# A two-layer decoder with mixtures of experts: routing two more sets of tokens inside the second layer's attentions, and another order of chunks and quads in the last layer

## The chip, the cores and the metric

The kernel runs on one core of a Trainium2 chip. The metric is the time of one execution on the device in microseconds (us). It has five engines that work side by side, each with an instruction queue of its own: the matrix engine (PE; its weight loads are listed as PEld), the vector engine (DVE), the scalar engine (ACT), GpSimd (POOL) and the sync engine (SP), which here issues DMA transfers. ACT and POOL issue DMA transfers as well.

## The reference

A decoder of two layers works on 32 sequences of 128 tokens with 128 features (4096 tokens), beside a context of the same shape. Each layer adds three things to x in turn: self-attention, cross-attention to the context, and a feed-forward part. The change touches the feed-forward part of the second layer, a mixture of 16 experts of which every token uses 4, and a shared expert that all tokens use:

```python
router_logits = x @ gate_w.T
biased = router_logits + expert_bias
_, sel = lax.top_k(biased, TOP_K)                       # TOP_K = 4, E = 16
raw = jnp.take_along_axis(router_logits, sel, axis=-1)
rw = jax.nn.softmax(raw.astype(jnp.float32), axis=-1).astype(x.dtype)
g = jnp.zeros((T, E), x.dtype).at[jnp.arange(T)[:, None], sel].add(rw)
for e in range(E):
    routed = routed + g[:, e:e + 1] * _swiglu(x, w1[e], w2[e], w3[e])
out = (_swiglu(x, sw1, sw2, sw3) + routed).reshape(B, S, Hd)
```

Here x is the layer-normalized input, and `_swiglu` is silu(x w1) times (x w3), times w2. Everything is in float32.

## The kernel before

The 4096 tokens stay in on-chip memory as x in 8 *groups* of 512 (4 *batches* of 128 each). Two groups make a *set*, so there are four sets: 0 (groups 0, 1), 1 (2, 3), 2 (4, 5) and 3 (6, 7).

**Two ways through the experts.** Sets 0, 2 and 3 (`SETS`) are *sorted by expert*. For each token and each of its 4 experts the place of a row in a table in device memory is worked out (`Tables.route`, `placed`, `owned`). POOL scatters the rows there with indirect DMAs (`way_out`, line 2096, 32 for a set). The table has 48 tiles of 128 rows, worked on four at a time as 12 *quads* for each set, 36 in all: `rows_of` loads rows and the weights of the tiles' experts (SP; the table holds at most three quads' weights on chip), `rows_turned` transposes (tile prows), `rows_up` makes pg and pu and `rows_down` makes pyrows, which go back to device memory. Then POOL gathers the rows (`way_back`, tile back, 32 gathers for a set), and `added` adds them to x on DVE. Set 1, the *dense pair* of groups, goes through all 16 experts and the shared one instead: 17 *chunks* a group, 34 in all. A chunk is `chunk_up` (pg, pu, Silu on ACT, two products on DVE, the second with the token's *shares* of the expert, loaded by `fetched`) and `chunk_down` (y). For the six groups of the sorted sets one chunk each remains, the shared expert (`alone`). The last chunk of a group transposes x into y as well and stores the output.

**Stages before that.** A group is normalized by `norm` (statistics on DVE, line 1115, and r on POOL, lines 1097 and 1098) and `scaled` (line 1126), transposed by `turn` into the tile hx, and a set's logits are made by `routing`. `route` and `choose`/`chosen` go on with the choice of experts a few instructions at a time; for the dense pair `send` stores the shares in device memory.

**Where the order comes from.** `steps` (line 1188) lists stages with the step they begin at, how many steps lie between two runs of a stage, and how many runs there are. Each step goes through the first list in order; instructions of the stages in `between` are put in one by one after each of theirs. The order is fixed for PE, DVE, ACT and POOL, in the last layer for SP too. `second_layers` (line 2528 and on) has both attentions of the second layer interleaved over all groups; group g leaves the cross-attention at step 17 + 4g, the last at step 45. In it set 0 is normalized, routed and scattered too (`way_out` from step 35 on, one batch of 4 scatters a step). `last_layer` (line 2108 and on) does everything else: the dense pair's and set 2's norms, turns and routing in steps 0 to 5, quads from step 1 on, chunks from step 6 on (one in each step until step 23, then in every second one), then steps with two chunks, then those that stand alone. The dictionary `at` holds which chunks stand at which step.

Of the kernel before, what the change touches and what calls it, by code (L numbers as in the profile page):

```python
# [9 lines left out]
F32 = mybir.dt.float32  # L10
# [945 lines left out]
def fast_decoder(ctx: ExitStack, tc: tile.TileContext, ins, spans, out: bass.AP):  # L956
# [847 lines left out]
    def mixture(tag, W, route, per, last, weights_of, kept=lambda g: None):  # L1804
# [13 lines left out]
        def turn(wk, g):  # L1818
            pool = edge if g in groups(0) else wk
            hs[g] = pool.tile([128, GT], F32, name="hx", bufs=2 if g in groups(0) else 5)  # L1820
            by_feature(xn.pop(g), hs[g])

        def routing(wk, n):
# [4 lines left out]
            choices[n] = route(lg, edge)  # L1828
# [74 lines left out]
        made = {"hs": hs, "combs": combs, "weights": weights, "NS": NS}  # L1903
# [56 lines left out]
    class Tables:  # L1960
# [32 lines left out]
        def kept(self, g):  # L1993
            self.xn[g] = self.spare[:, g]
            return self.xn[g]
# [97 lines left out]
        def way_out(self, n, u):  # L2093
            b, g = u % GB, n * NBR // GB + u // GB
            for k in range(4):
# [12 lines left out]
    def last_layer(tag, W, stages, of_expert, tables):  # L2108

        wk = phase(tag, mixture_psum)  # L2110
        tables.later(wk)
        send, made = stages[5], stages[-1]
        hs, shares, NS = made["hs"], {}, made["NS"]
        xn, places, parts, owners = tables.xn, tables.places, tables.parts, tables.owners
        factors, choices, held, ys, sgs, outs = ({} for _ in range(6))
# [5 lines left out]
        def scaled(g):  # L2121
            xn[g] = wk.tile([128, GB, D], F32, name="xr", bufs=6)
            yield from normed(wk, g, *factors.pop(g), xn[g], nc.vector)

        def turn(g):
            hs[g] = wk.tile([128, GT], F32, name="hx", bufs=NG - 2)
            by_feature(xn[g], hs[g])
# [10 lines left out]
        def routing(n):  # L2138
# [4 lines left out]
            choices[n] = tables.route(lg, n) if n in SETS else route_softmax(lg, edge)  # L2143
            next(choices[n])

        def chosen(n):
            comb = yield from choices.pop(n)
            if comb is not None:
                made["combs"][n] = comb
# [100 lines left out]

        at, todo = {}, list(dense)
        for s in range(6, NQ + 1):
            if s < 2 * QUADS or s % 2 == 0:
                at[s] = [todo.pop(0)]
        for s in range(NQ + 2, 100):
            if not todo:
                break
            at[s] = [todo.pop(0) for _ in range(min(2, len(todo)))]
        for k in range(0, 4, 2):
            at[s + k // 2] = alone[k : k + 2]  # L2260
        at[s + 3], at[s + 5] = alone[4:5], alone[5:6]
        LAST = s + 6
# [3 lines left out]
        for before, g in zip([None, *dense_groups], dense_groups):  # L2266
            for j in range(E // NS):
                fetches.append(((g, j), 5 if before is None else step_of[before, NS * j + NS - 1] + 1))
# [11 lines left out]
        def downs(s):  # L2280
            while waiting and (len(at.get(s, ())) < 2 or not at.get(s + 1)):
# [6 lines left out]
        def several(stage, keys):  # L2288
            def run(_):
# [5 lines left out]
        dense_n = ({1, 2, 3} - set(SETS)).pop()  # L2295
        n2, n3 = SETS[1:]
        batches = lambda n: [(n, u) for u in range(NBR)]
        once = lambda stage, k, s: (lambda _: stage(k), s, 1, 1)
# [3 lines left out]
            (each(rows_turned, quads), 1, 1, NQ),  # L2302
            (several(turn, of_set(dense_n)), 2, 1, 1),
            once(routing, dense_n, 2),
            (lambda _: send(wk, dense_n), 4, 1, 1),
            (several(turn, of_set(n2)), 4, 1, 1),
            once(routing, n2, 4),
            once(tables.owned, n2, 8),
            (several(turn, of_set(n3)), 10, 1, 1),
            once(routing, n3, 10),  # L2310
            once(tables.owned, n3, 14),
            (ups, 0, 1, LAST),
            (each(rows_down, quads), 2, 1, NQ),
            (each(rows_up, quads), 1, 1, NQ),
# [3 lines left out]
                (each(rows_of, quads[2:]), 1, 1, NQ - 2),  # L2318
# [360 lines left out]
```

## Time and profile before

| what | us |
|---|---|
| median of 3 runs (lowest, highest) | 1415.12 (1402.57, 1415.6) |
| the profiled execution's own time | 1410.02 |
| its span, first to last instruction | 1408.2 |
| mean granted clock of PE in it | 0.947 |
| busy in the span: PE, DVE, ACT, POOL | 1259.3, 858.3, 577.2, 534.6 |
| last instruction chain's largest shares | PE 64%, DVE 15%, POOL 7%, DMA 5% |
| bytes moved by DMA | 129.06 MB |

The profile is one execution. An engine is busy while one of its instructions runs; matmuls are pipelined and their ends are modelled. A matmul in float32 stands as two records in the profile. The granted clock is the share of its full clock that PE was given. DMA share is the mean busy share of the core's 16 DMA engines. A line such as "engine line waited for" gives the total of the waits, how many there were, and the longest. In the chain each line has its start, its length, and the engine, tile and line.

### The profile page before, as it was taken

What the parts mean: (1) busy time and instruction counts of PE and PEld (TensorE: products, weight loads), DVE (VectorE), ACT (ScalarE), POOL (GpSimd) and SP (SyncE); (2) the same over time, 40 slices, a digit from 0 to 9 for tenths busy, and PEclk for the clock granted to TensorE, in tenths of its full rate; (3) what the DMA queues carried; (4) which work ended last, traced back from release to release, by engine and by line L of the source; (5) the groups of instructions that cost most, each with busy time, mean ns of one, the idle gap of its engine ahead of it and who ended that gap; (6) DMA issues with size and microseconds to landing.
All of it is one profiled execution on the core that took longest, in us unless ns stands there. A gap on an engine that the chain in (4) does not pass through costs nothing.

```text
span 1408.2 us, 27520 instructions
## 1 busy us (share of the span) xinstructions
PE 1259.3 (89%) x10753; PEld 846.7 (60%) x10753; DVE 858.3 (61%) x2271; ACT 577.2 (41%) x848; POOL 534.6 (38%) x729
## 2 busy tenths in 40 slices
PE   3689999999999999699999988989986688799997
PEld 2357777777777787444444445656653376577753
DVE  5646767676777575385775536666674346534563
ACT  1354445454554433133232235555543434334432
POOL 5233243435341231032000214444427605575775
PEclk8789999999999999799999999989987869999999
DMA  9501111121111111455055020000001259599943
GB/s 351 177 1 32 32 31 33 32 50 34 41 31 32 32 32 37 92 112 122 14 107 122 0 97 1 3 1 2 2 1 31 84 156 334 193 337 306 326 147 96
DMA packets 89528, 129.06 MB, mean 92 GB/s; under 512 B 9872, under 2 KB 63760, under 8 KB 87984
## 3 DMA queue, kind: packets, MB, share of 16 engines
q1 hardware_dynamic: 76624, 102.59, 26.0%
q0 software_dynamic: 6144, 12.60, 3.0%
q10 hardware_dynamic: 6624, 12.05, 2.3%
q8 instruction: 87, 1.43, 0.4%
q14 instruction: 49, 0.40, 0.1%
HBM read 99.34 MB, written 27.85 MB: 90 GB/s over the span
## 4 chain that ended last, share of the span: by engine, by line
PE 64%; DVE 15%; POOL 7%; DMA 5%; ACT 4%; issue 3%; SPq 1%; DVEq 0%; ACTq 0%; POOLq 0%
PE po L977 8%; PE pg L977 7%; PE pu L977 7%; PE y L977 6%; PE pqk L977 6%; PE scores L977 4%; PE sums L977 4%; PE xscores L977 3%; POOL rows_in L2096 3%; PE pval L977 3%; DMA factor<-factors 2%; PE pyrows L977 2%; PE proj L977 2%; PE xsums L977 2%; PE qkvr L977 2%
## 5 line engine op out<-in xcount | busy, mean ns | idle before, releaser
L1280 ACT ACTIVATE e<-scores 128x1024 f32<-128x1024 f32 x128 | 124.0, 1021 | 61.5 <-PE scores L977 61.5
L977 PE MATMUL y<-sg,wide 128*128 128x512 f32 x224 | 117.6, 613 | 7.5 <-DVE sg L2229 2.6
L977 PE MATMUL pg<-hx,wide 128*128 128x512 f32 x224 | 116.0, 599 | 0.0
L977 PE MATMUL pu<-hx,wide 128*128 128x512 f32 x224 | 115.3, 596 | 0.0
L2204 POOL DMA_INDIRECT back<-rows_out,place x96 | 93.1, 970 | 37.5 <-issue 24.6
L1295 DVE STREAM_TRANSPOSE by_token<-sums 128x512 f32<-128x512 f32 x64 | 45.6, 713 | 96.7 <-PE sums L977 96.5
L1126 POOL TENSOR_SCALAR xn<-x,mv,r 128x128 f32<-128x128 f32 x80 | 67.7, 853 | 91.7 <-PE pxn L1135 82.8
L1097 POOL TENSOR_SCALAR r<-mv 128x4 f32<-128x4 f32 x48 | 11.5, 241 | 219.4 <-DVE mv L1116 219.0
L1531 ACT ACTIVATE e<-xscores 128x1024 f32<-128x1024 f32 x64 | 62.0, 1021 | 79.9 <-PE xscores L977 79.9
L1882 ACT ACTIVATE sg<-pg 128x512 f32<-128x512 f32 x72 | 43.0, 597 | 119.4 <-PE pg L977 110.4
L977 PE MATMUL sums<-e,v 128*32 128x128 f32 x2048 | 74.8, 290 | 17.2 <-POOL v L1075 17.1
L977 PE MATMUL scores<-qb,k 32*128 32x512 f32 x512 | 79.1, 689 | 11.9 <-ACT qb L1466 4.5
L1883 DVE TENSOR_TENSOR sg<-sg,pu 128x512 f32<-128x512 f32 x72 | 49.3, 685 | 61.1 <-PE pu L977 58.1
L1097 POOL TENSOR_SCALAR r2x<-mv 128x2 f32<-128x2 f32 x16 | 3.7, 234 | 212.0 <-DVE mv L1116 212.0
L977 PEld LDWEIGHTS sums<-e,v 128*32 128x32 f32 x2048 | 55.7, 115 | 46.8 <-POOL v L1075 21.6
L2096 POOL DMA_INDIRECT rows_in<-xr,place x64 | 62.9, 983 | 34.6 <-issue 18.0
L1545 DVE COPY v<-pval 128x512 f32<-128x512 f32 x64 | 43.5, 680 | 51.1 <-PE pval L977 51.1
L1579 ACT COPY av<-po 128x512 f32<-128x512 f32 x64 | 37.5, 586 | 89.6 <-PE po L977 89.5
L977 PEld LDWEIGHTS pu<-hx,wide 128*128 128x128 f32 x224 | 42.6, 191 | 52.5 <-issue 50.1
L977 PE MATMUL po<-e,v 128*64 128x128 f32 x1024 | 65.8, 281 | 8.2 <-DVE v L1545 8.2
L977 PE MATMUL po<-av,wide 128*128 128x256 f32 x256 | 64.1, 405 | 8.1 <-DVE av L1599 8.1
L977 PEld LDWEIGHTS y<-sg,wide 128*128 128x128 f32 x224 | 35.9, 189 | 58.0 <-DVE sg L1885 36.7
(300 smaller groups left out, 2913.2 us busy)
## 6 DMA issues: line engine op xcount, KB each, us to landing
row_weights<-in_w1f_dram SPq DMA_DIRECT2D x144, 192.0 KB, 4.2
factor<-factors SPq DMA_DIRECT2D x64, 256.0 KB, 5.0
share<-combined SPq DMA_DIRECT2D x32, 512.0 KB, 11.4
rows_in<-in_few SPq DMA_DIRECT2D x36, 256.0 KB, 4.1
rows<-rows_in SPq DMA_DIRECT2D x36, 256.0 KB, 5.3
rows_out<-yrows ACTq DMA_DIRECT2D x36, 256.0 KB, 4.3
share<-combined SPq DMA_DIRECT2D x8, 1024.0 KB, 7.8
wide<-in_w1f_dram SPq DMA_DIRECT2D x1, 3272.0 KB, 10.5
```

The source lines that it names most:

```text
L977: last[0] = nc.tensor.matmul(*args, **kw)
L1097: nc.gpsimd.tensor_scalar(t, src, add, None, ALU.add)
L1126: eng.tensor_scalar(n[:, b, :], x[g][:, b, :], mv[:, b, 0:1], r[:, b : b + 1], ALU.subtract, ALU.mult)
L1280: nc.scalar.activation(e[-1], ps[:, bass.ts(n, 2)].rearrange("p c i s -> p (c i) s"), AF.Exp, scale=scale)
L1295: nc.vector.transpose(tt.rearrange("p i t r -> p (i t r)"), po.rearrange("p i s -> p (i s)"))
L1531: nc.scalar.activation(e[-1], ps[:, n].rearrange("p r c s -> p (r c) s"), AF.Exp, scale=scale)
L1545: nc.vector.tensor_copy(v[:, bass.ts(n, XC), :], pv)
L1579: nc.scalar.copy(avs[w][n][:, :, bass.ts(b, S)], po)
L1882: nc.scalar.activation(sg, pg, AF.Silu)
L1883: nc.vector.tensor_tensor(sg, sg, pu, ALU.mult)
L2096: sent = nc.gpsimd.indirect_dma_start(out=rows_in[n], out_offset=bass.IndirectOffsetOnAxis(ap=self.places[n][:, k, u : u + 1], axis=0), in ...
L2204: nc.gpsimd.indirect_dma_start(out=outs[n, u][:, k], out_offset=None, in_=rows_out[n], in_offset=bass.IndirectOffsetOnAxis(ap=places[n][:, ...
```

## The change

Five things change.

1. In `second_layers` the stages `rnorm`, `rscaled` and `rturn` run for groups 0 to 5 and not only 0 and 1 (steps 18 + 4g to 20 + 4g); `routing` runs for sets 0, 1 and 2 (steps 25, 33, 41), the dense pair's choice is completed in steps 34 to 39 and sent at step 41. Turned inputs of groups 2 to 5 are kept in four context tiles that are no longer read (`cx`), and set 2's normalized rows in two more.
2. The scatters of set 0 go three to a step over steps 35 to 45, not four to a step over 35 to 42.
3. In `last_layer` the stages of 1 are gone for sets 1 and 2, except for set 2's choice and places (steps 0, 1) and its scatters, now two batches a step from step 2 on. Set 3's norm, turn, routing and scatters stand at steps 3 to 16.
4. The order of chunks: two in each of steps 0 to 2, one in each of steps 3 to 8, one in every second step from 9 to 29; the quads begin at step Q = 3. From step 40 on the other 11 chunks of the pair and four shared ones stand one to a step, and the two last shared ones at steps 55 and 59. The first shares are fetched at step 0, before the first quads' rows.
5. `downs` leaves two chunks waiting in steps 0 to 2 and 40 to 57. The last set's gathers stand at every second step.

```diff
-    def mixture(tag, W, route, per, last, weights_of, kept=lambda g: None):
+    def mixture(tag, W, route, per, last, weights_of, more={}, kept=lambda g: None):
...
-            pool = edge if g in groups(0) else wk
-            hs[g] = pool.tile([128, GT], F32, name="hx", bufs=2 if g in groups(0) else 5)
+            pool, bufs = (edge, 2) if g in groups(0) else (wk, 5)
+            hs[g] = more[g] if g in more else pool.tile([128, GT], F32, name="hx", bufs=bufs)
...
         def kept(self, g):
-            self.xn[g] = self.spare[:, g]
-            return self.xn[g]
+            if g < 2:
+                self.xn[g] = self.spare[:, g]
+            elif g * GB // NBR in SETS:
+                self.xn[g] = cx[g - 2].rearrange("p (b f) -> p b f", f=D)
+            return self.xn.get(g)
...
         def scaled(g):
-            xn[g] = wk.tile([128, GB, D], F32, name="xr", bufs=6)
+            xn[g] = wk.tile([128, GB, D], F32, name="xr", bufs=2)
...
-            hs[g] = wk.tile([128, GT], F32, name="hx", bufs=NG - 2)
+            hs[g] = wk.tile([128, GT], F32, name="hx", bufs=2)
...
+        Q = 3
+        many = {**{s: 2 for s in range(Q)}, **{s: 1 for s in range(Q, Q + 6)}, **{s: 1 for s in range(Q + 6, Q + 28, 2)}}
         at, todo = {}, list(dense)
-        for s in range(6, NQ + 1):
-            if s < 2 * QUADS or s % 2 == 0:
-                at[s] = [todo.pop(0)]
-        for s in range(NQ + 2, 100):
-            if not todo:
-                break
-            at[s] = [todo.pop(0) for _ in range(min(2, len(todo)))]
-        for k in range(0, 4, 2):
-            at[s + k // 2] = alone[k : k + 2]
-        at[s + 3], at[s + 5] = alone[4:5], alone[5:6]
-        LAST = s + 6
+        for s, n in many.items():
+            at[s] = [todo.pop(0) for _ in range(n)]
+        END = NQ + Q + 1
+        for s, item in enumerate(todo + alone[0:4], END):
+            at[s] = [item]
+        at[s + 1], at[END + 19] = alone[4:5], alone[5:6]
+        LAST = END + 21
...
         def downs(s):
-            while waiting and (len(at.get(s, ())) < 2 or not at.get(s + 1)):
+
+            while len(waiting) > (2 if s < Q or END <= s < LAST - 3 else 0):
                 chunk_down(*waiting.pop(0))
                 yield
...
-            (each(rows_turned, quads), 1, 1, NQ),
-            (several(turn, of_set(dense_n)), 2, 1, 1),
-            once(routing, dense_n, 2),
-            (lambda _: send(wk, dense_n), 4, 1, 1),
-            (several(turn, of_set(n2)), 4, 1, 1),
-            once(routing, n2, 4),
-            once(tables.owned, n2, 8),
-            (several(turn, of_set(n3)), 10, 1, 1),
-            once(routing, n3, 10),
-            once(tables.owned, n3, 14),
+            (each(rows_turned, quads), Q, 1, NQ),
+            (several(turn, of_set(n3)), 6, 1, 1),
+            once(routing, n3, 6),
+            once(tables.owned, n2, 3),
+            once(tables.owned, n3, 11),
...
-                once(chosen, n2, 5),
-                once(several(norm, of_set(n3)), None, 5),
-                once(tables.placed, n2, 6),
-                *((each(tables.way_out, batches(n2)[i::2]), 7, 1, 4) for i in range(2)),
-                once(several(scaled, of_set(n3)), None, 8),
-                once(chosen, n3, 11),
-                once(tables.placed, n3, 12),
-                (each(tables.way_out, batches(n3)), 13, 1, NBR),
-                (each(way_back, batches(0)), 21, 1, NBR),
-                (each(added, batches(0)), 24, 1, NBR),
+                once(chosen, n2, 0),
+                once(tables.placed, n2, 1),
+                (each(tables.way_out, to_send(n2, 2)), 2, 1, 4),
+                once(several(norm, of_set(n3)), None, 3),
+                once(several(scaled, of_set(n3)), None, 4),
+                once(chosen, n3, 7),
+                once(tables.placed, n3, 8),
+                (each(tables.way_out, to_send(n3, 1)), 9, 1, NBR),
+                (each(way_back, batches(0)), 19, 1, NBR),
+                (each(added, batches(0)), 22, 1, NBR),
...
-                (each(way_back, batches(n3)), NQ + 3, 1, NBR),
-                (each(added, batches(n3)), NQ + 5, 1, NBR),
+                (each(way_back, batches(n3)), END + 1, 2, NBR),
+                (each(added, batches(n3)), END + 4, 2, NBR),
...
-            (first(rturn), 20, 4, R),
+            (first(rturn), 20, 4, 3 * R),
...
-            (first(routing), 25, 1, 1),
+            (first(routing), (25, 33, 41), 1, 3),
             (lambda _: tables.owned(0), 36, 1, 1),
+            (lambda _: send(early, 1), 41, 1, 1),
...
-                (first(rscaled), 19, 4, R, xturn),
-                (first(rnorm), 18, 4, R),
+                (first(rscaled), 19, 4, 3 * R, xturn),
+                (first(rnorm), 18, 4, 3 * R),
...
-                (lambda u: tables.way_out(0, u), 35, 1, NBR),
+                (lambda i: tables.way_out(0, to_send[3 * i : 3 * i + 3]), 35, 1, 11),
+                (lambda _: choose(1, 3), 34, 1, 6),
...
-        mixture1 = mixture("l1f", W1F, lambda lg, _: tables.route(lg, 0), 1, True, of_expert, tables.kept)
+        route = lambda lg, n: tables.route(lg, n) if n in SETS else route_softmax(lg, edge)
+        mixture1 = mixture("l1f", W1F, route, 1, True, of_expert, {2: cx[0], 3: cx[1], 4: cx[4], 5: cx[5]}, tables.kept)
```

## What was predicted

> **What bounds the kernel now.** I read the page first, then busy time by stretches, then the chain of work that ended last, then the waits. On the page the matrix engine is busy for most of the span:
>
> ```profile
> PE 1259.3 (89%) x10753; PEld 846.7 (60%) x10753; DVE 858.3 (61%) x2271; ACT 577.2 (41%) x848; POOL 534.6 (38%) x729
> ```
>
> That is an average over stages with different limits. The same figures by stretches of layer 1 (columns: stretch, its length, busy time of each engine, granted clock, DMA share, GB/s):
>
> ```profile
> core 0: us, PE busy (x) PEld busy (x) DVE busy (x) ACT busy (x) POOL busy (x), PEclk, DMA share, GB/s
> 830.00:1038.00 208.00, 190.79 (x2394) 126.45 (x2394) 139.46 (x392) 112.13 (x157) 90.89 (x138) 0.96 0.01 2
> 1038.00:1069.00 31.00, 24.37 (x284) 16.11 (x284) 20.58 (x58) 9.76 (x12) 10.73 (x14) 0.78 0.04 13
> 1069.00:1117.00 48.00, 26.99 (x345) 15.23 (x345) 18.98 (x61) 19.45 (x22) 36.92 (x48) 0.86 0.12 38
> 1117.00:1165.00 48.00, 39.27 (x231) 35.45 (x224) 20.31 (x83) 17.07 (x25) 3.73 (x7) 0.68 0.59 175
> 1165.00:1207.00 42.00, 38.82 (x238) 28.97 (x237) 25.71 (x83) 17.95 (x29) 25.60 (x28) 1.00 0.91 327
> 1207.00:1222.00 15.00, 7.70 (x49) 5.98 (x50) 5.20 (x16) 3.17 (x5) 8.46 (x9) 0.91 0.22 66
> 1222.00:1290.00 68.00, 66.91 (x388) 48.70 (x388) 27.02 (x50) 26.90 (x46) 42.76 (x44) 0.97 0.97 321
> 1290.00:1352.00 62.00, 60.60 (x412) 48.99 (x411) 37.68 (x86) 27.16 (x46) 45.51 (x48) 1.00 0.95 307
> 1352.00:1408.00 56.00, 45.85 (x148) 23.25 (x146) 29.00 (x64) 13.64 (x23) 36.17 (x37) 0.96 0.29 83
> ```
>
> The attentions end about 1117 (steps 33 to 45 are 1038 to 1117); the last layer follows. Until 1038 PE is the limit. From 1038 to 1117 nothing is full: PE is busy 51 of 79 us. The last layer opens badly (1117 to 1165: clock 0.68, DMA 0.59) and has a hole at 1207 to 1222 (DMA 0.22), where the second set's rows are still being scattered. From 1222 to 1352 the DMA engines are full (0.97, 0.95). The chain shows a step of that stretch, one quad and one chunk:
>
> ```profile
> 1250.97 0.89 PE pyrows L977 x8
> 1251.86 0.89 PE pg L977 x8
> 1252.76 0.89 PE pu L977 x8
> 1253.65 0.86 PE y L977 x2
> 1254.95 0.86 PE pg L977 x2
> 1256.66 0.89 PE pyrows L977 x8
> ```
>
> A chunk is pg, pu and y: 3 x 0.86 = 2.58 us. A quad is its transposes (0.44, what is left between y and pg) and 3 x 0.89: 3.11. Together 5.69, the distance of the two pyrows. In the waits of 1038 to 1118, PE stands behind POOL's queue, which the scatters fill:
>
> ```profile
> PEld sums L977 <- POOL v L1075: 10.8, 6, 3.9
> PE pxn L1135 <- POOL xn L1126: 5.2, 1, 5.2
> ```
>
> **Part 1: what moves into the attentions.** For each of groups 2 to 5, from the timeline: statistics 4 x (0.26 + 0.18) = 1.8 us of DVE; r 0.23 + 1.04 = 1.3 of POOL; normalizing 0.6 of DVE and 1.6 of POOL (in the last layer it was 1.1 of DVE); four transposes 0.66 of PE and a copy 0.58 of ACT. Twice the logits: 1.85 of PE at full clock, 3.60 at half. The dense pair's routing: 3.9 of DVE in some 18 instructions and one Exp; send: 0.9 of PE at full clock, two copies of 0.57, two small DMAs. Sum: PE 4 x 0.66 + 2 x 1.85 + 0.9 = 7.2 (13 at half clock), DVE 4 x 2.4 + 3.9 = 13.5, POOL 4 x 2.9 = 11.6, ACT 3.8. Not all is new there: twelve statistics run at 1075 to 1081, where the attention's own norm has four, so eight of the last layer (3.5 of DVE, 2.6 of POOL) were already ahead of its start, in front of the r that the 5.2 us wait of pxn hangs on.
>
> Groups 2 and 3 fall into steps 26 to 32, where PE is the limit (191 of 208): two turns there cost 1.3; DVE and POOL have a third and a half of the time free and hide the rest. In steps 33 to 45 come groups 4 and 5, both logits, the routing and send: PE 5.9, of which I put 3 on the path, as PE idles a third of the time; DVE 2 x 2.4 + 3.9 - 3.5 = 5.2, put on the path whole, because the norms stand in DVE's queue ahead of the transposes that PE waits for. POOL: 5.8 - 2.6 added, but at 3 scatters a step instead of 4, steps 35 to 42 carry 24 instead of 32, 8 x 1.26 less (spacing of scatters, 0.96 and 0.3 issue). A quarter of the 16 us of waits behind POOL goes: -4. Sum 1.3 + 3 + 5.2 - 4 = +5. Bounds: -8 (POOL's relief alone, half of its waits) to +27 (PE at half clock and DVE, all on the path). The attentions then end at 1122. The last scatters of set 0 now end after the attentions (steps 43 to 45), but the first rows are wanted only in step 3.
>
> **Part 2: the opening.** Steps 0 to 2 are six chunks, 15.5 us of PE that wait for no rows. They need the shares: four fetches of 1 MB, now ahead of the quads on SP, with two quads of 1.05 MB: 6.3 MB. At the rate of a full DMA, (64.0 MB moved from 1117 to 1352 over 195 us of share, 0.329 MB/us), 19 us. The last layer's first 48 us now have a clock of 0.68. How long a low clock lasts (the same columns):
>
> ```profile
> 1146.00:1157.40 11.40, 11.31 (x52) 10.19 (x53) 0.29 (x1) 4.23 (x7) 0.00 (x0) 0.50 0.20 48
> ```
>
> PE was busy all the 11.4 us and stayed at half. Again so: +5.7, 21 us in all. Beneath it DVE does the second set's routing and places (5.0 of work at 1153 to 1166, 6 for set 0's places at 1038 to 1049), 11 us, and six chunks' products, 6 x 1.38: 19 us, just hidden; what DVE holds up there is the second set's scatter, which then starts about 24 us in, ends 8 x 5.04 = 40 later at 64, and is wanted at step 13 (21 + 40 + 4 x 5.1 = 81). The hole at 1207 goes; this slack of 17 us is the cover. A rule of the Trainium skill (TensorE: Matmul & The Clock Gate, Part 1) says that about 3.4 us of sustained work restores the clock; by it the 5.7 would be 1.7, 4 us less. The row above disagrees, and the sum goes by the row.
>
> **Part 3: the middle.** Steps 3 to 8, a quad and a chunk each: 6 x 5.69 = 34, and the third set's turn and logits 3.2 and two placings of 1.9: 41; I write 40. DMA there: 10 MB, 30 us, so PE binds. Steps 9 to 38 hold 30 quads and 11 chunks: PE 30 x 3.11 + 11 x 2.58 = 122. DMA: a quad moves 0.79 of weights, 0.26 in and 0.26 out, 1.31 MB; 30 of them 39.3, shares 4.2, one scatter and two gathers of 2.1 each: 49.8 MB, 151 us. DMA binds, so the quads without chunks near the end (steps 31 to 38) run at about 4.8 (1.31 and a gather's 0.26 MB at 0.329) and not at 3.11. Last quad: 21 + 40 + 151 = 212. Counting otherwise, 195 us of DMA share plus 13 in which PE holds it up: 208. I take 210 after 1122; before it was 235 after 1117. Bounds: 186 (PE alone, with no DMA wait: 17 + 41 + 122 + 6 for what is added to x) and 224 (the hole's 15 us comes back). The Trainium skill (DMA: Bandwidth & Descriptors, Anatomy of one DMA) gives transfers a slope of 436 GB/s; by it 49.8 MB would take 114 us and PE would bind at 122, 29 us earlier. This trace at full share shows 329, and 393 at most in any ten us.
>
> The second group's share fetches wait on SP for their buffer, with quad loads behind them; before, SP's waits on shares were 5.9 us in all, covered by two quads loaded ahead. Nothing is charged.
>
> **Part 4: the end.** After the last quad stand 17 chunks instead of 15: 43.9, and x's transposes 8 x 0.89 = 7.1: 51.0 of PE (before 45.8, from 1352 to 1398). From there to the end were 10.5: last gather, sum, copy, store. So 61.5. POOL alone: rows stored 4.3, 32 gathers 40.3, 9 from the last one's end: 53.6, under it. Keeping chunks two behind costs nothing: Silu 0.60 and two products of 0.69 lie under the next two chunks' 3.4 of pg and pu.
>
> **Sum.** 1122 + 210 + 61.5 = 1393.5 of span, 1395 with the 1.8 around it, against 1410.0 of the profiled execution. The three runs lie on both sides of that (1402.6 to 1415.6, median 1415.1), so I carry no shift: 1395.
>
> **Rivals.**
> - DMA does not bind and the clock opens fast (the 186): 1122 + 186 + 61.5 + 1.8 = 1371. For it: ten-us stretches with 393 GB/s. Against: 130 us at 0.96 share.
> - The gain is hidden: DVE's queue puts all moved work on the path (+27 instead of +5), or the second set's scatter starts over 17 us late and the hole returns (+14): 1409 to 1417. For it: DVE is in order and holds products that wait for shares.
> - The other side: PE stands 5 us more often in steps 33 to 45, because turns and logits in PE's queue wait for POOL's normalizing behind scatters. Each such stand drops the clock: 5 + 5.7 = 10.7. Two eat the gain, four make it slower by 1% (1395 + 43 = 1438). For it: the waits of pxn and sums above, and 0.78 and 0.86 of clock. Against: POOL has less to do in these steps.
>
> **How the numbers follow.** Under 1401 or over 1429 is what a measurement of this kernel can tell from no change. Forecast 0.50 (own range 1380 to 1408); first rival 0.14; second 0.20; third 0.16. Under 1401: three quarters of the forecast, the first rival and a little of the second, 0.55. Over 1429: most of the third, 0.15. Between: 0.30. The range leaves out a third of the first rival below (0.05) and what is over 1430 (0.15): 1368 to 1430.
>
> **What would show it.** Right: pg<-hx of group 2 ahead of any prows; DMA share near 0.95 from the opening to the last quad with no hole; last quad about 210 after the attentions' end; that end within 1114 to 1149. Wrong: first scatter of set 2 later than 40 us in; PE under half busy in steps 33 to 45; quads of steps 31 to 38 at 3.1 apart (then DMA was no bound).

## The result and the profile after

| | before | after |
|---|---|---|
| median of 20 runs each (us) | 1415.32 (1402.57 to 1421.91) | 1422.58 (1410.38 to 1430.83) |
| ratio, 95% interval | | 1.0059 (1.0032 to 1.0086) |
| the profiled execution: its own time, span, granted clock | 1410.02, 1408.2, 0.947 | 1417.03, 1414.8, 0.954 |
| attentions of layer 1, from the first pkphi to the last proj with w1x | 294.4 | 298.1 |
| from there to the last pyrows, the last quad's end | 231.8 | 232.2 |
| from there to the end of the span | 56.3 | 57.3 |

The kernel became 0.6% slower; 1.1% faster was forecast against the profiled execution (1395 for 1410.02). The time lies in the stated range (1368 to 1430), but the forecast gain of the last layer is not there: it takes 289.5 us after the attentions, 288.1 before.

The first line of the page is as good as unchanged; busy time doesn't tell where the gain went:

```profile
PE 1259.1 (89%) x10753; PEld 843.4 (60%) x10753; DVE 852.7 (60%) x2263; ACT 575.3 (41%) x846; POOL 539.8 (38%) x737
```

The stretches of the last layer tell it. The attentions now end at 1125.3 (same columns as before: stretch, length, busy time of five engines, granted clock, DMA share, GB/s):

```profile
core 0: us, PE busy (x) PEld busy (x) DVE busy (x) ACT busy (x) POOL busy (x), PEclk, DMA share, GB/s
1125.00:1148.00 23.00, 19.53 (x52) 10.16 (x53) 14.04 (x39) 6.38 (x9) 5.64 (x7) 0.85 0.86 304
1148.00:1161.00 13.00, 12.51 (x66) 8.35 (x65) 10.37 (x33) 4.15 (x7) 9.39 (x10) 1.00 0.65 215
1161.00:1181.00 20.00, 11.54 (x63) 8.74 (x61) 4.42 (x12) 4.12 (x7) 15.86 (x18) 0.74 0.64 218
1181.00:1200.00 19.00, 17.72 (x113) 13.59 (x113) 10.77 (x36) 8.69 (x14) 8.73 (x9) 1.00 0.59 182
1200.00:1247.00 47.00, 44.19 (x300) 35.70 (x298) 17.92 (x37) 20.01 (x34) 31.56 (x33) 1.00 0.98 323
1247.00:1310.00 63.00, 57.56 (x371) 47.26 (x372) 26.41 (x56) 24.82 (x42) 34.28 (x37) 0.95 0.93 293
1310.00:1350.00 40.00, 30.02 (x222) 25.68 (x221) 14.48 (x36) 13.62 (x24) 25.58 (x27) 1.00 0.97 313
1350.00:1358.00 8.00, 7.15 (x45) 6.34 (x44) 4.01 (x10) 2.52 (x5) 0.00 (x0) 0.79 0.27 100
1358.00:1415.00 57.00, 50.04 (x158) 25.33 (x156) 28.97 (x59) 14.63 (x25) 31.54 (x32) 0.97 0.25 75
```

The opening (1125 to 1148) is near what was foreseen, clock 0.85 and DMA 0.86 where before had 0.68 and 0.59. From 1200 to 1350, when the quads' loads are nearly over, the DMA engines are full (0.93 to 0.98), also as foreseen. In between is a new hole: for 52 us, from 1148 to 1200, DMA moves at 0.59 to 0.65, and in its middle PE is busy 11.5 of 20 us at a clock of 0.74, while POOL is busy 15.9. The old hole at 1207 to 1222 is gone, and this one stands in its place.

What POOL does there, and who waits, is in the timeline of that stretch (start, length, engine, line, operation; in brackets the idle time before it and what ended it):

```profile
1156.89 0.18 DVE L1116 BATCH_NORM_AGGREGATE mv<-parts 128x2 f32<-128x6 f32 x1
...
1168.33 0.96 POOL L2100 DMA_INDIRECT rows_in<-ctx,place  x1 [0.30 <-issue]
1169.31 0.26 POOL L1097 TENSOR_SCALAR r<-mv 128x4 f32<-128x4 f32 x1
1169.65 1.05 POOL L1098 TENSOR_TENSOR r<-r,half 128x4 f32<-128x4 f32 x1
...
1170.73 1.12 DVE L1126 TENSOR_SCALAR xr<-x,mv,r 128x128 f32<-128x128 f32 x4 [9.48 <-POOL r L1098]
...
1173.86 0.69 DVE L2232 TENSOR_TENSOR sg<-sg,share 128x512 f32<-128x512 f32 x1
...
1174.61 1.22 PE L977 MATMUL y<-sg,wide 128*128 128x512 f32 x1 [8.46 <-DVE sg L2232]
```

Read it from the top. Set 3's norm (step 3) has its statistics on DVE by 1157.1. The next thing it needs, r, is two instructions on POOL, 1.3 us together for a group. They are queued behind set 2's scatters, two batches a step since step 2, and scatters follow each other every 1.26 us: r begins at 1169.3, 12 us after its input was ready. Its reader, `scaled` of step 4, is one step behind `norm`, so DVE reaches it early and stands 9.5 us for it. DVE's order is fixed, and behind `scaled` stand the chunks' products, the first of which follows it at 1173.2: y has no sg, PE stands 8.5 us. Then quads come late, their buffers come free late, and SP's weight loads wait for pyrows, 14.8 us at the longest. The same as totals of waits from 1125 to 1360 (engine, line, what it waited for: us in all, how many, the longest):

```profile
DVE xr L1126 <- POOL r L1098: 9.7, 2, 9.5
PE y L977 <- DVE sg L2232: 9.4, 2, 8.5
```

In before, set 3's `norm` stood at step 5, ahead of set 2's scatters (from step 7 on), and `scaled` at step 8, three steps after it.

### The profile page after: what moved, and what is told of

It is laid out like the page before. It is cut to its first block, busy times and chain, and to the rows that moved or that the text cites. A ratio compares the mean times of both kernels' runs of the same rounds, so it can differ in the third digit from the quotient of the medians.

```text
span 1414.8 us, 27530 instructions
## 1 busy us (share of the span) xinstructions
PE 1259.1 (89%) x10753; PEld 843.4 (60%) x10753; DVE 852.7 (60%) x2263; ACT 575.3 (41%) x846; POOL 539.8 (38%) x737
## 4 chain that ended last, share of the span: by engine, by line
PE 62%; DVE 16%; DMA 8%; POOL 5%; ACT 4%; issue 3%; SPq 1%; DVEq 0%; ACTq 0%; POOLq 0%
PE po L977 8%; PE pg L977 7%; PE pu L977 6%; PE y L977 6%; PE pqk L977 6%; PE scores L977 5%; PE sums L977 4%; DMA row_weights<-in_w1f_dram 4%; PE xscores L977 3%; PE pval L977 3%; DMA factor<-factors 2%; PE proj L977 2%; PE xsums L977 2%; ACT e L1280 2%; PE qkvr L977 2%
## 5 line engine op out<-in xcount | busy, mean ns | idle before, releaser
L1126 POOL TENSOR_SCALAR xn<-x,mv,r 128x128 f32<-128x128 f32 x84 | 71.1, 854 | 91.3 <-PE pxn L1135 82.7
L977 PE MATMUL pg<-hx,wide 128*128 128x512 f32 x152 | 78.0, 595 | 0.0
L977 PE MATMUL pu<-hx,wide 128*128 128x512 f32 x152 | 77.7, 593 | 0.0
L2192 DVE TENSOR_TENSOR sgrows<-sgrows,pu 128x512 f32<-128x512 f32 x36 | 24.7, 687 | 86.2 <-PE pu L977 85.4
L1579 ACT COPY av<-po 128x512 f32<-128x512 f32 x64 | 37.6, 587 | 89.0 <-PE po L977 88.9
L1510 DVE COPY qk<-pqk 128x512 f32<-128x512 f32 x64 | 43.4, 685 | 41.1 <-PE pqk L977 40.9
## 6 DMA issues: line engine op xcount, KB each, us to landing
wide<-in_w1f_dram SPq DMA_DIRECT2D x1, 3272.0 KB, 10.7
```

The source lines that it names most:

```text
L977: last[0] = nc.tensor.matmul(*args, **kw)
L1126: eng.tensor_scalar(n[:, b, :], x[g][:, b, :], mv[:, b, 0:1], r[:, b : b + 1], ALU.subtract, ALU.mult)
L1510: nc.vector.tensor_copy(t, ps)
L1579: nc.scalar.copy(avs[w][n][:, :, bass.ts(b, S)], po)
L2192: nc.vector.tensor_tensor(sg, sg, pu, ALU.mult)
```

## The experiments

**The theory** after this comparison: the middle is bound by DMA as predicted, and the loss is the queue in front of r. **Its rivals**: the DMA engines would have delivered the last quad no earlier without that stand; the attentions, not the last layer, eat the gain; the order of chunks is worth nothing.

Each edit is to the changed kernel unless it says otherwise. A count that orders all of them is the start of the copy `hrows` on ACT, one for each quad, in us after the attentions' end. It splits the time to the last pyrows into the prediction's terms: the first quad; quads 0 to 5 (steps 3 to 8); from quad 6 to the last quad's end.

| kernel | attentions | first quad | quads 0 to 5 | quad 6 to the last pyrows | last pyrows | end after it | ratio to before, 95% interval |
|---|---|---|---|---|---|---|---|
| predicted | +5 | 21 | 40 | 151 | 210 | 61.5 | |
| after | 298.1 | 23.5 | 53.2 | 155.5 | 232.2 | 57.3 | 1.0059 (1.0032 to 1.0086) |
| e1 norm first | 306.4 | 23.4 | 42.5 | 155.6 | 221.5 | 56.9 | 0.9968 (0.9932 to 1.0003) |
| e2 scaled late | 306.3 | 23.7 | 35.7 | 165.4 | 224.8 | 57.0 | 1.0013 (0.9974 to 1.0053) |
| e3 one batch a step | 302.1 | 23.7 | 43.2 | 154.1 | 221.0 | 56.9 | 0.9993 (0.9956 to 1.0031) |
| e4 four scatters | 301.3 | 21.8 | 54.6 | 154.3 | 230.7 | 57.0 | 1.0086 (1.0053 to 1.0119) |
| e5 few chunks first | 302.1 | 15.7 | - | - | 225.7 | 57.0 | 1.0006 (0.9969 to 1.0042) |
| e6 half the weight loads | 302.1 | 23.8 | 42.5 | 133.5 | 199.8 | 57.4 | 0.9805 (0.9744 to 0.9867) |
| e7 set 2 back | 303.1 | 32.4 | 49.8 | 154.8 | 237.0 | 57.0 | 1.0087 (1.0051 to 1.0123) |
| e8 spread | 306.3 | 23.7 | 43.2 | 153.2 | 220.1 | 57.8 | 0.9977 (0.9946 to 1.0009) |
| e9 before again | 291.0 | - | - | - | 232.8 | 56.1 | 0.9995 (0.9959 to 1.0032) |
| e10 even | 306.3 | 23.7 | 35.8 | 159.6 | 219.1 | 57.2 | 0.9957 (0.9928 to 0.9986) |
| e11 even, one batch | 306.4 | 23.5 | 37.2 | 158.7 | 219.4 | 57.4 | 0.9981 (0.9947 to 1.0015) |
| e12 norms later | 293.9 | 23.5 | 38.3 | 159.8 | 221.6 | 56.9 | 0.9981 (0.9943 to 1.0019) |

Times of stretches are of one profiled execution each; ratios are of 10 to 20 timed runs (4 for e6). A dash stands where the quads begin at other steps. The attentions' column differs by up to 8 us between kernels whose attentions are the same (after, e1 to e3, e5, e6, e8, e10, e11); the columns of the last layer are the ones to compare.

### e1: r ahead of the scatters

```diff
                 once(chosen, n2, 0),
+                once(several(norm, of_set(n3)), None, 0),
...
-                once(several(norm, of_set(n3)), None, 3),
```

> The changed kernel with one line moved: set 3's norm stands at step 0 of the last layer instead of step 3, so its r is in POOL's queue ahead of set 2's 32 scatters. Queue theory: in the changed kernel r ran at 1169, 12 us after its statistics, behind 16 scatters; DVE stood 9.5 us for it, PE 8.5 us behind DVE, then some 6 us at half clock, and SP's loads stood 14.8 us. All of that goes: the last quad comes 12 to 18 us earlier after the attentions' end (232 us becomes 214 to 220), the time falls by 10 to 18 us against the changed kernel, to 0.993 to 0.999 of the kernel before. Rival, DMA is the bound whatever waits: the hole closes, the same bytes are still in the way, the last quad stays within 4 us of 232 and the ratio within 0.003 of 1.006.

The same stretches, counted from the attentions' end of this kernel (1139.4):

```profile
1175.40:1195.40 20.00, 19.76 (x126) 15.08 (x125) 8.95 (x25) 8.89 (x15) 15.12 (x17) 1.00 0.93 297
1195.40:1214.40 19.00, 16.74 (x112) 13.29 (x111) 13.21 (x43) 8.05 (x14) 10.85 (x12) 1.00 0.81 275
```

In the first of these PE is busy 19.8 of 20 us at full clock instead of 11.5 at 0.74, and DMA is at 0.93 instead of 0.64, with POOL as busy as before (15.1): the scatters did not shrink, r only no longer stands behind them. Six quads take 42.5 us instead of 53.2, the last quad ends 10.7 us earlier, and nothing is given back after quad 6 (155.6 and 155.5). It is a little less than the 12 to 18 us expected. Where one stage of two groups stands in a queue is worth 0.9% of the whole kernel.

### e2 and e3: the same stand taken away in two other ways

In e2 r stays behind the scatters, but set 3's readers come four steps later. In e3 the scatters are thinned to one batch a step.

```diff
-                once(several(scaled, of_set(n3)), None, 4),
+                once(several(scaled, of_set(n3)), None, 8),
```

> The changed kernel with set 3's norm left at step 3 (its r still behind 16 scatters on POOL), but what reads r moved from step 4 to step 8, with turn and logits at step 10 and choice, places and scatters 4 steps later too. Queue theory: r is as late as before, but by step 8 it is there, so neither DVE nor PE waits; the gain is that of the run with the norm first, within 4 us, if the third set's later scatters (steps 13 to 20) don't collide with set 0's gathers from step 19 on. Rival, it is the scatters themselves that slow everything beside them (DMA or descriptors): r is no matter, and the stretch of the 32 scatters stays as slow as in the changed kernel, ratio about 1.006.

```diff
-                (each(tables.way_out, to_send(n2, 2)), 2, 1, 4),
+                (each(tables.way_out, to_send(n2, 1)), 2, 1, NBR),
```

> The changed kernel with set 2's scatters at one batch (4) a step over steps 2 to 9 instead of two batches a step over 2 to 5; the norm stays at step 3. Queue theory: 8 scatters and not 16 stand before r, 10 us less of POOL's queue (8 x 1.26), so r comes about when its statistics are done plus 2 us, and DVE's wait falls from 9.5 us to under 2; most of the gain of the run with the norm first, 8 to 16 us against the changed kernel. But the scatters of set 3 stand at step 9 and may queue. Rival, DMA is the bound: no change from 1.006.

(e2 moves set 3's turn, choice, places and scatters by four steps too.) In e2, two lines of the tile view, of r and of its reader (count, min/median/max ns, first and last start):

```profile
L1126 DVE TENSOR_SCALAR xr<-x,mv,r x8: 340/341/455, 1190.0 to 1195.0; 128x128 f32<-128x128 f32 x8
L1097 POOL TENSOR_SCALAR r<-mv x2: 218/237/256, 1181.4 to 1182.8; 128x4 f32<-128x4 f32 x2
```

r is late as ever, 44.5 us after the attentions' end (1136.9), against 44.0 in after, and nobody waits for it; quads 0 to 5 take 35.7 us. So it is not the late r that costs, but a reader in DVE's queue before r can be there. After quad 6, where set 3's stages now stand, e2 takes 9.8 us more than e1, more than the 6.8 gained on e1 before it. In e3 r begins 34.1 us after the attentions' end, no wait for it is listed, and the last quad comes out as in e1 (221.0). Three edits that have only the end of the stand in common move the last quad by 7 to 11 us; that settles its cause, and the rival "DMA would have been no earlier" falls. In the timed runs e1 and e3 lie clear of after; e2's interval overlaps after's, so for e2 only the profile shows the gain.

### e4: the first set's scatters four to a step again

```diff
-                (lambda i: tables.way_out(0, to_send[3 * i : 3 * i + 3]), 35, 1, 11),
+                (lambda i: tables.way_out(0, to_send[4 * i : 4 * i + 4]), 35, 1, 8),
```

> The changed kernel with one part undone: set 0's scatters four to a step over steps 35 to 42, as before, not three to a step over 35 to 45. Theory of the prediction (POOL's queue holds PE up in these steps): with 8 more scatters in steps 35 to 42 the attentions end 4 to 10 us later than in the changed kernel (1125), at 1129 to 1135; the ratio goes from 1.006 to 1.008 to 1.013. Rival, DVE and the chain of norm, r and normalizing set the pace there, scatters fill gaps: the end moves by under 2 us.

Waits of PE's weight loads in the attentions' last 85 us, of after and then of e4:

```profile
PEld sums L977 <- POOL v L1075: 4.4, 4, 2.1
```

```profile
PEld sums L977 <- POOL v L1075: 9.3, 5, 3.9
```

The waits behind POOL come back (before had 10.8), and the time from the last pkphi to the attentions' end is 90.5 us instead of 87.7; in the other eight profiles with the same attentions it is 87.8 or 87.9. These 2.8 us are near the -4 of the prediction; the 4 to 10 expected were too much. The last layer takes 1.8 of them back (287.7 us for 289.5). The ratio is 0.0027 above after's, 3.8 us, but the two intervals overlap, so the timed runs don't confirm a size.

### e5: the order of chunks

```diff
 on e1:
-        Q = 3
-        many = {**{s: 2 for s in range(Q)}, **{s: 1 for s in range(Q, Q + 6)}, **{s: 1 for s in range(Q + 6, Q + 28, 2)}}
+        Q = 1
+        many = {**{s: 1 for s in range(1, 18)}, **{s: 1 for s in range(18, 30, 2)}}
```

> The kernel with the norm first, with one part of the change undone: no six chunks ahead of the quads. Quads begin at step 1, one chunk stands beside each in steps 1 to 17, then one in every second step to 28, 11 and the shared ones from step 38 on as before. Theory of the prediction (the opening is worth having because PE has 15 us that wait for no rows): PE stands from the attentions' end until set 0's rows are there, and at half clock after it; the last quad comes 6 to 14 us later after the attentions' end than in the kernel with the norm first (221 us), ratio 1.001 to 1.007. Rival, DMA sets the last quad: the quads' loads start earlier, so the last quad comes as early or earlier (210 to 221), and the ratio is 0.990 to 0.998.

```profile
1128.00:1143.00 15.00, 0.49 (x2) 0.30 (x2) 7.22 (x32) 0.23 (x1) 8.24 (x12) 0.62 0.88 333
```

Here PE does nothing for 15 us after the attentions, waiting for the first quads, while DMA runs at 0.88. The six chunks that fill this time in e1 are 15.5 us of PE, and yet putting them there is worth only 4 us at the last quad (225.7 against 221.5), less than the 6 to 14 expected, while the rival's earlier last quad did not come either: PE's work is not what the middle is short of.

### e6: less for DMA to do

```diff
 on e1:
+                if q % 2 == 0:
                     nc.sync.dma_start(out=w.rearrange("p k f -> p (k f)"), in_=src)
+                else:
+                    at_e = spans["w1f"]["gud"][0] + 3 * (t % E) * S
+                    w = W.tile[:, at_e : at_e + 3 * S].rearrange("p (k f) -> p k f", k=3)
```

> The kernel with the norm first, but every second quad of the last layer loads no expert weights: it uses a fixed expert's from the copy that lies on chip, so 72 of the 144 loads of 192 KB (14 MB of 64.6) are left out; the matmuls are the same in number and size, the values not those of the right experts. If the DMA engines bind the middle: 14.2 MB at 0.329 MB/us are 43 us less, PE or POOL then bind; the last quad comes 185 to 200 us after the attentions' end instead of 221, and the time falls by 20 to 36 us (ratio 0.972 to 0.983). If POOL's 160 scatters and gathers (201 us) or PE's waits for DVE bind: the last quad stays within 8 us of 221, ratio over 0.990.

```profile
1197.00:1260.00 63.00, 61.66 (x428) 50.82 (x427) 23.91 (x47) 28.39 (x49) 44.17 (x47) 1.00 0.84 278
```

With half the weight loads gone PE is full (61.7 of 63) and DMA is not (0.84). The last quad ends 21.7 us earlier, at the upper end of the 185 to 200 expected, and all of it is gained after quad 6 (133.5 instead of 155.6); quads 0 to 5 take the same 42.5. So DMA bounds the middle after quad 6, and without these loads PE does, at 199.8; the prediction's lower bound, PE alone, was 186. The edit also leaves SP fewer loads to issue and fewer weight buffers to wait for, which no run separates; what speaks for the DMA engines themselves is their share, 0.93 to 0.98 in after.

### e7: set 2 routed in the last layer again, the dense pair left in the attentions

```diff
-                (first(rscaled), 19, 4, 3 * R, xturn),
-                (first(rnorm), 18, 4, 3 * R),
+                (first(rscaled), 19, 4, 2 * R, xturn),
+                (first(rnorm), 18, 4, 2 * R),
...
+                once(several(norm, of_set(n2)), None, 0),
+                once(several(scaled, of_set(n2)), None, 0),
+                once(several(norm, of_set(n3)), None, 1),
...
```

(Set 2's turns and logits at step 1, its choice at step 2, places at step 3 and scatters from step 4 on belong to the edit too; set 3's norm is at step 1.)

> The kernel with the norm first, with one part of the change undone: set 2's norms, turns and logits are again in the last layer (steps 0 and 1, its choice at step 2, places at 3, scatters at 4 to 7); only the dense pair is routed inside the attentions. It tells what set 2's move costs the attentions and brings the last layer. Theory: of the attentions' growth (from 294 to about 303 us, counted from 825 to 833) half belongs to set 2, whose norms and logits stand in steps 34 to 41 where DVE is in front of PE, so the attentions end 3 to 6 us earlier; the last layer loses 2.5 us of PE and 4 of DVE in its opening, hidden or not: ratio 0.992 to 0.998, about that of the norm first (0.997) or better. Rival, the scatter of set 2 now starts 12 us later and quad 12 waits: a hole again, ratio 1.002 to 1.008.

```profile
1165.00:1180.00 15.00, 9.94 (x54) 6.64 (x52) 12.42 (x43) 4.71 (x7) 0.12 (x1) 1.00 0.26 93
```

A hole comes back at once: DVE (12.4 of 15) works mostly on set 2's choice and places, set 2's first scatter starts 42.2 us after the attentions' end instead of 23.5 in e1, and DMA is at 0.26. It is the rival that the expectation named, and slightly more (1.0087 for 1.002 to 1.008). Against e1 the attentions are 3.3 us shorter and the last layer 15.6 longer (294.0 against 278.4); the ratios are 0.0119 apart, 17 us. With this order of chunks, moving set 2 into the attentions is what pays; moving the dense pair alone does not.

### e8: chunks spread to the end

```diff
 on e1 and e3:
-        many = {..., **{s: 1 for s in range(Q + 6, Q + 28, 2)}}
+        many = {..., **{s: 1 for s in range(Q + 6, Q + 35, 2)}}
```

(The chunks left waiting at the end follow the new count of steps, and set 3's scatters begin one step later.)

> The attempt at something faster: norm first, set 2's scatters one batch a step, and the chunk in every second step goes on to step 37, so four chunks move from the end into steps 31 to 37, where PE waits for the DMA engines a fifth to a quarter of the time. If DMA binds there, the four chunks (10.3 us of PE) cost under 2 us before the last quad, and the end after it shrinks from 57 us to what POOL's 32 gathers need, 53 to 54: 2 to 4 us less than norm first or one batch a step, ratio 0.990 to 0.997. Rival, PE binds there after all: the last quad moves out by 6 to 10 us and nothing or less is won, ratio 0.998 to 1.004.

Four more chunks beside quads (10.3 us of PE) cost the last quad nothing (220.1), as a middle bound by DMA should have it, but the end did not shrink (57.8). From the waits after the last quad:

```profile
POOL back L2207 <- DVE sg L2232: 11.2, 1, 11.2
...
PE y L977 <- DVE sg L2230: 8.8, 1, 8.8
```

Fewer chunks leave PE idle for 8.8 us, because POOL's gathers now set the end: the first begins 3.8 us after the last quad, 32 take 40.6, and 13.4 follow them. That is the bound that the prediction wrote down for POOL, 53.6 there and 57.8 here. In after it is as near: 3.8, 41.0 and 12.5, beside a PE that is busy 50.0 us. Taking work from PE alone brought nothing; taking gathers from POOL was not tried.

### e9: before once more

> The kernel before, once more, for a second profile of it. Its one profile so far has attentions of 294.4 us (from the first pkphi to the last proj<-in_w1x); nine profiles of the changed kernels have 298 to 306. If the moved work costs the attentions some +5 to +8, this one lies within 290 to 300. If it comes out at 302 or more, the profile of before was a lucky one, and the difference of the attentions is less than the spread of identical code. The last layer (attentions' end to the end) is 288 in either case, within 2, and the ratio 1.000 within its interval.

The attentions are 291.0 us here and 294.4 in the first profile. Nine profiles with the attentions of the changed kernel (after, e1 to e3, e5, e6, e8, e10, e11) have 298.1 to 306.4, 304.0 in the mean. PE's waits for normalized x (xn) in them are 16.5 us in both profiles of before and 22.2 to 22.5 in the nine. So the moved work does cost something there.

### e10 and e11: a better order

e10 keeps set 3's norm at step 0 and spreads the 17 chunks beside quads evenly. e11 has, in addition, the edit of e3.

```diff
 on e1:
-        many = {**{s: 2 for s in range(Q)}, **{s: 1 for s in range(Q, Q + 6)}, **{s: 1 for s in range(Q + 6, Q + 28, 2)}}
+        many = {**{s: 2 for s in range(Q)}, **{s: 1 for s in range(Q, Q + 34, 2)}}
```

> Set 3's norm at step 0 as in the run norm-first, and the 17 chunks that stood one a step in steps 3 to 8 and in every second step from 9 to 29 now stand in every second step from 3 to 35. In norm-first DMA is idle for 10.7 us in steps 3 to 8. Theory that PE binds there (six quads and six chunks by 5.69): three chunks less in those steps let DMA fill them, 5 to 8 us earlier at the last quad (214 to 217 us after the attentions' end, against 221.5), the end likewise, ratio 0.990 to 0.994. Rival, that what holds DMA back there is not PE's chunks but the ramp of the quads (pyrows that the weight loads wait for, the turn and the placing of set 3): last quad at 219 to 222, ratio 0.996 to 0.999.

> As the run even, and set 2's scatters one batch a step, from step 2 to 9, instead of two. It takes POOL's queue out of the way of the opening's chunks and ends the scatters later. If the scatters' traffic or POOL's queue still costs something in the opening, 2 to 4 us earlier than the run even; if not, the same last quad within 2 us; if the scatters are now too late for quad 12, a stand of DMA at about 60 us after the attentions' end and 3 to 8 us later.

e10 is faster than before by 0.4%, and by its interval the only version that is, beside e6, which leaves work out; its interval overlaps e1's, so that it beats e1 is shown by the profile alone. The last quad is 2.4 us earlier than in e1, at the rival's end of the expectation: quads 0 to 5 are 6.7 us shorter, so PE did bind there, but three chunks more stand beside later quads and take 4.0 back. e11's last quad is within 0.3 us of e10's; the scatters' place in POOL's queue no longer matters once nothing waits behind them.

### e12: where the attentions' cost lies

```diff
 on e10:
-                (first(rscaled), 19, 4, 3 * R, xturn),
-                (first(rnorm), 18, 4, 3 * R),
+                (first(rscaled), (19, 23, 28, 32, 36, 40), 1, 3 * R, xturn),
+                (first(rnorm), (18, 22, 27, 31, 35, 39), 1, 3 * R),
```

(The turns, both routings and the dense pair's choice move by one step as well.)

> As the run even, and in the attentions the norms, normalizing and turns of groups 2 to 5 one step later, so that they no longer share a step with the norm of another attention. In the changed kernel PE waits 22.4 us for xn in the attentions, in before 16.5; 5.6 of the difference is at two places, 992 and 1025 to 1028, where a moved norm shares the step. If those waits are what the moved work costs, they go: attentions 3 to 6 us shorter than the run even at a like clock, ratio 0.990 to 0.994. Rival: the moved work delays whatever norm is next on DVE and POOL, and the waits turn up one step on: the waits for xn stay within 2 us of 22.4, ratio 0.994 to 0.998.

PE's waits for normalized x in the attentions, of e10 and then of e12:

```profile
PE pxn L1135 <- POOL xn L1126: 11.9, 9, 4.1
PE pxn L1135 <- DVE xn L1126: 10.4, 6, 5.1
```

```profile
PE pxn L1135 <- POOL xn L1126: 7.9, 6, 4.0
...
PE pxn L1135 <- DVE xn L1126: 4.4, 4, 2.9
```

They fall by 10 us, below before's 16.5, so the moved norms did stand in front of others. The profile's attentions are 293.9 us, 12.4 less than e10's, but only 4.2 less than after's 298.1, and after's attentions are the same as e10's. And the ratio, 0.9981, is not below e10's 0.9957: of the gain that the profile shows, the timed runs show nothing. Their mean clock was 0.949 in e12 and 0.955 in e10. Whether the fuller PE lowers the clock that it is granted, or the two groups of runs, taken on different chips, drew differently, stays open.

## Why the prediction was wrong

**The failed step is in part 3: "Steps 3 to 8, a quad and a chunk each: 6 x 5.69 = 34 ... I write 40 ... so PE binds."** It measured 53.2. The 40 is right for the kernel it describes: e1, with r out of the scatters' queue, has 42.5. The 10.7 between them is one wait that the prediction did not price. Part 2 had followed POOL's 32 scatters through those steps, as lateness of the scatters themselves ("slack of 17 us is the cover"), and that was right too: they began 23.6 us after the attentions' end (foreseen 24) and quad 12 did not wait. But it did not ask what else is queued on POOL between them, r of set 3, nor who reads that one step later. The change had moved both `norm` into the burst of scatters and `scaled` next to it.

The rest of the miss at the last quad is as large, 11.5 us in small pieces: the first quad at 23.5 for 21; 42.5 for 40 even in e1; 155.5 for 151 from quad 6 on, where the sum had counted quads by their starts and the last quad's own way through (5 us) not at all. Together 232.2 for 212, of which I took 210. So the wait explains why the kernel became slower, but not the whole distance to the forecast: e1, without it, has a ratio of 0.9968, where 0.989 was forecast.

**Part 1, the attentions.** The sum starts from a misread end: it takes 1117 for before, where the last proj begins at 1120.1. So before's last quad came 231.8 us after that end, not 235. Predicted was +5. The pair of profiles has +3.7, the mean of the nine against that of before's two +11; the ratio of after is 8.3 us on the median, of which the last layer has 1.4, which leaves 7. The size holds within that spread, the place doesn't. I had put 3.7 of it into steps 33 to 45; there the time from the last pkphi to the end is 88.9 before (89.0 in e9) and 87.7 after. It lies earlier, in the steps where "DVE and POOL have a third and a half of the time free and hide the rest": PE's waits for xn grew from 16.5 to 22.4 us, at 992 and at 1025, in steps that hold a moved norm too, and e12 takes them away. Free time on average did not hide an instruction in front.

**Part 2, the opening**, came out at 23.5 us for 21, but not by its terms. The granted clock of 0.85 over these 23.5 us cost about 3.5, not 5.7. But PE stood 3.4 us for DVE's first mask of set 2's places, which the prediction had called "just hidden":

```profile
1134.11 0.51 PE L977 MATMUL places<-mask,in_last 128*128 128x144 f32 x2 [3.40 <-DVE mask L2018]
```

That the two errors partly cancel is luck.

**Part 3's bound** held: DMA at 0.93 to 0.98 from 1200 to 1350, and e6 shows that it binds. (Its "393 at most in any ten us" was read low: 1165.5 to 1175.5 of before moved 413 GB/s.) Of the rivals, the first (PE binds, 1371) falls by e6. The third, PE standing in steps 33 to 45, falls by the 87.7. The second, the gain hidden, came nearest; its price was 14 us for a hole, but its mechanism, set 2's scatters too late for their quads, was not the one at work. That the measured time lies in the stated range is owed to its part above 1417, which was kept for the third rival; it is no credit to the sum.

**Part 4**: 57.3 for 61.5. PE's work was sized rightly (50.0 busy, 51.0 predicted) and goes on to 1408.9; what follows it is the last copy and store, 5.9 us. The 10.5 that I added held the last gather and sum as well, and these lie beside PE's last chunks.

In sum on the profiled execution: attentions end 1125.3 for 1122, +3.3, nearly all of it the misread 1117; last quad +22.2; end -4.2: 21.3 us over the 1393.5, at 1414.8.

**The clock rule.** After its stand PE came back at half clock, once more in the middle of the layer:

```profile
1166.10:1174.60 8.50, 0.05 (x1) 0.00 (x0) 3.62 (x11) 0.01 (x1) 7.19 (x9) 0.69 0.78 286
1174.60:1178.00 3.40, 3.39 (x10) 2.24 (x10) 0.55 (x1) 0.42 (x1) 2.51 (x3) 0.50 0.18 60
...
1179.00:1180.00 1.00, 1.00 (x9) 0.94 (x7) 0.00 (x0) 0.60 (x2) 0.69 (x2) 0.72 0.11 37
1180.00:1181.00 1.00, 1.00 (x12) 1.00 (x11) 0.00 (x0) 0.00 (x0) 0.89 (x1) 1.00 0.19 66
```

Busy from 1174.6, it got the full clock back in the stretch from 1179 on, after about 5 us at half, which cost some 2.5 us on top of the 8.5 of the stand; together that is about e1's 10.7. The Trainium skill (TensorE: Matmul & The Clock Gate, Part 1) gives about 3.4 us of sustained work, and says that the window runs freely. This place is nearer to it than the 11.4 us by which the prediction went. But those 11.4 us are not of one kind either: until 1153.0 of before PE works on small products, transposes and logits 16 columns wide, and from the next pyrows on it takes 4.8 us:

```profile
1146.10:1153.00 6.90, 6.90 (x33) 5.75 (x33) 0.00 (x0) 2.32 (x4) 0.00 (x0) 0.50 0.03 7
1153.00:1157.80 4.80, 4.80 (x23) 4.80 (x24) 0.29 (x1) 2.31 (x3) 0.00 (x0) 0.50 0.50 126
1157.80:1158.80 1.00, 0.85 (x8) 0.61 (x6) 0.48 (x1) 0.27 (x2) 0.00 (x0) 0.99 1.03 374
```

Whether narrow work fails to bring the clock back is not shown: no run varies it, and in the opening of after PE was busy 7.9 us, from 1134.1 to 1142.0 (0.57 in the mean), before the clock was full again. None of the three is a price to count on.

## What to carry to other kernels

When a burst of long instructions (scatters, here) is moved on an in-order queue, list every small instruction that now stands between or behind them, and for each the step of its first reader on another in-order engine: the cost is not the burst but the reader, and everything queued behind the reader. Put the producer ahead of the burst, thin the burst, or put the reader several steps back; each took away the stand here (e1, e3, e2). In a stage bound by DMA look for pauses of the transfers first: closing one was worth 10.7 us here, while 15.5 us of PE work beside them was worth 4 (e5) and 10.3 us nothing (e8).

## What was not expected of the hardware

The spread of single runs goes with the granted clock. In 107 runs of the kernel before, taken beside the experiments, spans follow the mean granted clock (0.939 to 0.957, correlation -0.94): 12.5 us for each 0.01, about what 0.01 of 0.946 makes of PE's 1259 busy us (13.3). Identical attentions took 298.1, 302.1 or 306.4 us in different profiles, in steps of about 4 us, by which 20-us stretches got a clock of 1.00 and which got 0.8 to 0.95. A gain of some us in one profile pair is therefore no evidence alone; e12 is the example.

A scatter or gather through POOL holds its queue for 1.25 us, about 0.95 of its own and 0.30 before the next, with DMA full (0.98) or not (0.25): from the first to the last of 32 it took 39 to 45 us.
